# A graph network on one core: layer 1 loads its slot rows and block places in halves of a group instead of quarters

## The chip, the cores and the metric

The kernel runs on one core of a Trainium2 chip. The metric is the device time of one execution in microseconds. The engines named below are TensorE (PE; PEld is its weight load), VectorE (DVE), ScalarE (ACT), GpSimd (POOL) and SyncE (SP), which here only issues DMAs.

## The reference

Two graph layers over 12,500 nodes of 32 channels and 400,000 edges, sorted by destination. Layer 0 weighs each source row with nine spline coefficients from the edge's two attributes and with `weight`, and takes the mean over a node's edges; layer 1 weighs it with four coefficients from the edge's type and sums. After each layer the input is added and the row normalised.

```python
def reference(x, src, dst, edge_attr_2, edge_type_8, ...):
    # layer 0
    messages = einsum('ek,ei,kio->eo', basis(edge_attr_2), x[src], weight)
    out = zeros.at[dst].add(messages) / max(degree, 1)[:, None]
    x = layernorm(x + out + x @ root_w.T + root_b)
    # layer 1
    out = sum over b of segment_sum((x[src] @ W[b]) * etw[b][edge_type][:, None], dst)
    return layernorm(x + out)
```

## The kernel before

The edges are cut into 125 groups of 2304 (`NG`, `GE`) and a rest of near tiles. In a first phase (to about 690 us) each group's edges are sorted by source, so that the rows of one stretch of 896 nodes (a block: 7 windows of 128 nodes) lie next to one another. There are `NBL` = 14 blocks in a group. For every block the sort leaves two things in DRAM: a row of 608 int16 slot numbers (`slots`: which node of the window a slot wants) and a place (`begin_d`, written by `counted`: where the block's rows go among the group's 2304 edges).

Then each layer (`layer(0)`, `layer(1)`) runs over the groups. `take(g)` fetches a group's source rows without a gather, block by block:

- `block(k)` loads, at the first block of each of four `PIECES` of 3, 4, 3 and 4 blocks, the piece's slot rows into `sl`, broadcast to 128 partitions (L1312, on SP's queue), and its places into `hd` (L1316, SP's queue as well). ScalarE loads the places into registers (L1318, a TENSOR_LOAD).
- VectorE compares `sl` with the partition's number and makes the one-hot `s` of the piece (L1324).
- TensorE multiplies seven windows of node rows with `s` into one of three PSUM banks (L1334), 98 matmuls a group.
- ScalarE copies the bank to its place in `yt`, at an offset that it takes from the registers (L1341), 14 copies a group.

`use(g, yt)` of the group before runs between the blocks, in three parts of six chunks. `product`: TensorE turns the rows (`y`, L1354, six matmuls), VectorE makes a one-hot of the destination (`hot`, L1366) and the row times its coefficients (`outer`, `last[0]`, L584 through the helper). `add`: TensorE adds them up in `agg` (L1389, six calls, two instructions each in f32), `LAG` = 2 parts later in layer 1. The sums go to `rows` through ScalarE (`agg_sb`, L603; `rows`, L591 and L593) and small matmuls (L609), and into the nodes in `some` (L743, L746). `Near` takes the rest of the edges by gathers on GpSimd (L124, `n_xg`) and matmuls (`n_bank`, L1083), in units of up to 28 gathers, spread over the groups.

Buffers: `srcs` holds 4 `sl` in layer 1 (2 in layer 0), `heads` 2 `hd`, `onehots` 5 `s` in layer 1, `prods` 4 `hot` and `products` 4 `outer`. The `y` of two parts and the column numbers that `hot` reads lie in one PSUM bank.

The order of the instructions on each engine is not that of the source: when the program is built, a scheduler lays out every engine's queue by priorities and assumed durations, within the dependences and the few orders that the source sets (`tc.issue_after`). Each engine, and SP's queue of DMAs, then works through its queue in order.

Of the kernel before, what the change touches and what calls it, by code (L numbers as in the profile page):

```python
# [11 lines left out]
I16 = mybir.dt.int16  # L12
I32 = mybir.dt.int32
# [4 lines left out]
P = 128  # L18
# [4 lines left out]
def kernel(  # L23
# [38 lines left out]
    nc = tc.nc  # L62
# [3 lines left out]
    CH, NG, G0 = 18, 125, 33  # L66
# [29 lines left out]
    NBL = NW // B  # L96
# [13 lines left out]
    dram = ctx.enter_context(tc.tile_pool(name="dram", bufs=1, space=bass.MemoryType.DRAM))  # L110
# [21 lines left out]
    sort = phase0.enter_context(tc.tile_pool(name="sort", bufs=1))  # L132
# [45 lines left out]
    row = const.tile([P, 1], F32)  # L178
# [47 lines left out]
    def wide(name="wg"):  # L226
        return node_ps.tile([P, 4 * P], F32, name=name)
# [216 lines left out]
    WS = off_[B]  # L444
# [11 lines left out]
        signs(src_16, thr[:NG, w:w + 1], -1.0, counts[:NG, w:w + 1])  # L456

    PIECES = [(k * NBL // 4, (k + 1) * NBL // 4) for k in range(4)]
    PB = max(k1 - k0 for k0, k1 in PIECES)
    PW = PB * WS  # L460
    assert PB <= 4
    PAD = 512
    begin_d = dram.tile([NG, NBL, 4], I32, name="begin_d")
    seg = dram.tile([NG * NBL, 2], F32, name="seg")
    ROWS = TG * NBL
    NT = (NG + TG - 1) // TG
# [11 lines left out]
    def counted():  # L478
        nc.vector.tensor_scalar(counts[:NG, 1:NW], counts[:NG, 1:NW], 0.5, GE / 2, op0=ALU.mult,
                                op1=ALU.add)  # L480
        nc.vector.memset(counts[:, :1], 0.0)
        nc.vector.memset(counts[:, NW:], float(GE))
        out_, t = [sort.tile([P, NBL, B], F32, name=n) for n in ("outside", "rel_to")]
        far = sort.tile([P, 2], F32, name="far")
        firsts, ends = [counts[:NG, i:i + NW].rearrange("g (b j) -> g b j", j=B) for i in (0, 1)]
        anchors = firsts[:, :, BL:BL + 1].to_broadcast([NG, NBL, B])

        for c, to, f, op in ((firsts, out_, lo, ALU.is_lt), (ends, t, hi, ALU.is_gt)):
            nc.vector.tensor_tensor(to[:NG], c, anchors, op=ALU.subtract)
            nc.vector.tensor_tensor(to[:NG], to[:NG],  # L490
                                    f[:NG, None, :].to_broadcast([NG, NBL, B]), op=op)
        nc.vector.tensor_tensor(out_[:NG], out_[:NG], t[:NG], op=ALU.add)
        nc.vector.tensor_reduce(far[:NG, :1], out_[:NG].rearrange("g b j -> g (b j)"), axis=AX.X, op=ALU.add)
        far_ps = wide()
        nc.tensor.matmul(far_ps[:1, :1], far[:NG, :1], ones[:NG, :1], start=True, stop=True)
        nc.vector.tensor_tensor(unfit, unfit, far_ps[:1, :1], op=ALU.add)
        place = sort.tile([P, NBL], F32, name="place")
        nc.vector.tensor_tensor(place[:NG], firsts[:, :, 0], firsts[:, :, BL], op=ALU.subtract)
        nc.vector.tensor_scalar(place[:NG], place[:NG], float(AHEAD), 0.0, op0=ALU.add, op1=ALU.max)
        nc.vector.tensor_scalar(place[:NG], place[:NG], float(AHEAD), None, op0=ALU.min)  # L500

        nc.vector.scalar_tensor_tensor(place[:NG], firsts[:, :, 0], float(BANK), place[:NG],
                                       op0=ALU.mult, op1=ALU.add)
        p_i = sort.tile([P, NBL, 4], I32, name="p_i")
        nc.gpsimd.memset(p_i, 0)
        for k0, k1 in PIECES:
            n = k1 - k0
            nc.vector.tensor_copy(p_i[:NG, k0:k1, :n],
                                  place[:NG, None, k0:k1].to_broadcast([NG, n, n]))
        nc.sync.dma_start(begin_d.rearrange("g b i -> g (b i)"),  # L510
                          p_i[:NG].rearrange("g b i -> g (b i)"))
        sg = sort.tile([P, NBL, 2], F32, name="sg")
        nc.vector.tensor_scalar(sg[:NG, :, 0], firsts[:, :, BL], edges[:NG], None, op0=ALU.add)
        nc.vector.tensor_copy(sg[:NG, :, 1], node[:NG, :NW:B])
        nc.vector.tensor_scalar(sg[:NG, :, 1], sg[:NG, :, 1], row[:NG], None, op0=ALU.subtract)
        nc.sync.dma_start(seg.rearrange("(g b) i -> g (b i)", b=NBL),
                          sg[:NG].rearrange("g b i -> g (b i)"))
        nc.vector.memset(begin, 0.0)
        for t in range(NT):
            n = min(ROWS, NG * NBL - t * ROWS)  # L520
            nc.sync.dma_start(begin[:n, t, :], seg[t * ROWS:t * ROWS + n, :])
# [652 lines left out]

    def layer(which):

        NSRC, NONE, NOUT, LAG, NSUM = ((2, 3, 3, 1, 14), (4, 5, 4, 2, 18))[which]
        KK = K if which == 0 else NB
        GF = G0 if which == 0 else 0
        parts = x3[which][0]  # L1180
        with ExitStack() as stack:
            srcs = stack.enter_context(tc.tile_pool(name="srcs", bufs=NSRC))
# [3 lines left out]
            heads = stack.enter_context(tc.tile_pool(name="heads", bufs=2))  # L1186
# [112 lines left out]
            def take(g):  # L1299

                yt = yts[g % NYT]
                begins = {}
                ones_of = {}

                def block(k):
                    for k0, k1 in PIECES:
                        if k == k0:
                            n = (k1 - k0) * WS
                            sl = srcs.tile([P, PW], I16, name="sl")
                            r0 = g % TG * NBL  # L1310
                            a = slots[g // TG][r0 + k0:r0 + k1, :]
                            nc.sync.dma_start(sl[:, :n], bass.AP(tensor=a.tensor, offset=a.offset,  # L1312
                                                                 ap=[[0, P], [1, n]]))

                            hd = heads.tile([1, 4], I32, name="hd")
                            nc.sync.dma_start(hd, begin_d[g:g + 1, k0, :])  # L1316
                            with tc.issue_after(moves[-2].ins) if len(moves) > 1 else ExitStack():
                                _, v = nc.values_load_multi_w_load_instructions(  # L1318
                                    hd[:, :k1 - k0], engines=[mybir.EngineType.Activation],
                                    min_val=0, max_val=GE * BANK + AHEAD,  # L1320
                                    skip_runtime_bounds_check_because="counted, and bounded")
                            begins.update(zip(range(k0, k1), v))
                            s = ones_.tile([P, PW], BF16, name="s")
                            nc.vector.tensor_scalar(s[:, :n], sl[:, :n], row, None,  # L1324
                                                    op0=ALU.is_equal)
                            for i in range(k0, k1):
                                ones_of[i] = s[:, (i - k0) * WS:]
                    s = ones_of.pop(k)
                    bank = banks[(g * NBL + k) % len(banks)]
                    for j in range(B):  # L1330
                        a, b = at_[j]
                        w = k * B + j

                        nc.tensor.matmul(bank[:, AHEAD + a:AHEAD + b], parts[:, w * M3:w * M3 + P],  # L1334
                                         s[:, off_[j]:off_[j + 1]], start=(j == 0),
                                         stop=(j == B - 1), skip_group_check=True)
                    v = begins.pop(k)
                    to, place = [nc.s_assert_within(
                        e, 0, top, skip_runtime_bounds_check_because="counted, and bounded")
                        for e, top in ((v >> 9, GE), (v & (BANK - 1), AHEAD))]  # L1340
                    moves.append(nc.scalar.activation(  # L1341
                        yt[:M3, ds(to, LONG)], bank[:M3, ds(place, LONG)], AF.Copy))
                return [lambda k=k: block(k) for k in range(NBL)], yt

            def use(g, yt):
# [77 lines left out]
            for g in range(GF, NG + 1):  # L1423
# [6 lines left out]
                n, m = len(new), len(left)  # L1430
# [68 lines left out]
    for c in range(0, CH, 4):  # L1499
        n = min(4, CH - c)  # L1500
# [11 lines left out]
    ends[0][2].append(fallen)  # L1512
    phase0.close()
    layer(0)
    phase1.close()
    ends[1][2].append(near_fits)
    layer(1)
    again = const.tile([1, 1], I32)
    nc.vector.tensor_scalar(again, unfit, 0.5, None, op0=ALU.is_gt)
# [157 lines left out]
```

## Time and profile before

| | |
|---|---|
| median of 12 runs | 3684.37 us (3674.16 to 3696.37) |
| the profiled execution | 3690.56 us, span 3688.5 us |
| granted TensorE clock, mean | 0.915 |
| busy share of the span: PE, PEld, DVE, ACT, POOL | 78%, 67%, 82%, 58%, 70% |
| layer 0 | about 700 to 2300 us |
| layer 1 | about 2310 to 3650 us |
| `sl` loads | 868: 434 of 608 KB, 434 of 456 KB |
| `hd` loads | 868 |

The rows of the profile name line, engine, operation, what is written and what is read. "Idle before" is time in which the engine did nothing before the instruction, and the name behind the arrow is what ended it. An idle engine that is not the bound costs nothing.

### The profile page before, as it was taken

Reading aid. Unit: us, or ns where it says so; the run is one execution under the profiler, and the core shown is the slowest. Engines: PE = TensorE matmul, PEld = TensorE weight load, DVE = VectorE, ACT = ScalarE, POOL = GpSimd, SP = SyncE. Lnnn points to the kernel's source line nnn. Section 1 sums busy time; section 2 is a strip of 40 time slices with the busy share of each in tenths; the row PEclk is TensorE's granted clock in tenths of the full one; section 3 lists DMA queues with packets and bytes.
Section 4 is the critical chain, followed back from the end, with each engine's and each line's share of the span. In section 5 each row is a group of like instructions: output and inputs, shape, how many; then the busy total and the mean of one; then the engine's idle time right before and its main releaser. Section 6 shows DMA issues by size and latency. Waiting matters only on the chain.

```text
span 3688.5 us, 112981 instructions
## 1 busy us (share of the span) xinstructions
PE 2859.7 (78%) x40674; PEld 2463.0 (67%) x40674; DVE 3008.9 (82%) x5850; ACT 2145.3 (58%) x5610; POOL 2590.1 (70%) x2395
## 2 busy tenths in 40 slices
PE   2222221159999999999999998889999999999997
PEld 1121111147877787777777776788888888888886
DVE  5899989579999998887777776678888788888886
ACT  4688866336666665555565654455555555555553
POOL 4767777727777777777777773577777777777730
PEclk9995555579999999999999998899999999999998
DMA  4000000145555555554555544577777676777662
GB/s 94 14 11 14 14 14 14 31 165 173 171 167 174 170 175 154 160 165 148 157 165 154 154 153 150 174 221 228 227 230 222 215 225 220 225 226 229 215 219 89
DMA packets 266157, 565.07 MB, mean 153 GB/s; under 512 B 83608, under 2 KB 149756, under 8 KB 265086
## 3 DMA queue, kind: packets, MB, share of 16 engines
q1 hardware_dynamic: 187288, 511.82, 41.3%
q0 software_dynamic: 75888, 40.38, 7.9%
q8 instruction: 319, 5.23, 0.6%
q10 hardware_dynamic: 2410, 5.59, 0.6%
q14 instruction: 252, 2.06, 0.2%
HBM read 531.77 MB, written 25.78 MB: 151 GB/s over the span
## 4 chain that ended last, share of the span: by engine, by line
PE 45%; POOL 13%; issue 7%; DVE 7%; ACT 5%; DMA 3%; ACTq 1%; SPq 0%; DVEq 0%; POOLq 0%
PE agg L1389 23%; PE bank L1334 15%; POOL n_xg L124 13%; ACT yt L1341 3%; PE y L1354 2%; DVE outer L584 2%; PE n_bank L1083 2%; DMA n_xg<-in_x_dram,n_idx 1%; PE wg L880 1%; DVE s L1324 1%; DVE hot L1366 1%; PE n_sum L746 1%; PE wg L609 1%; ACT agg_sb L603 1%; DVE hot L1376 1%
## 5 line engine op out<-in xcount | busy, mean ns | idle before, releaser
L124 POOL DMA_INDIRECT n_xg<-in_x_dram,n_idx x1469 | 1638.0, 1115 | 559.5 <-issue 433.1
L1341 ACT ACTIVATE yt<-bank x3038 | 1163.5, 383 | 544.0 <-PE bank L1334 244.7
L1389 PE MATMUL agg<-hot,outer 128*128 128x82 f32 (+1 forms) x7812 | 1400.6, 324 | 9.3 <-DVE hot L1376 8.6
L1334 PE MATMUL bank<-s,x 128*128 128x108 bf16 (+3 forms) x21266 | 1162.0, 202 | 103.7 <-ACT yt L1341 70.7
L124 POOL DMA_INDIRECT n_xg<-z_dram,near_i x875 | 921.4, 1053 | 365.8 <-issue 258.5
L1389 PEld LDWEIGHTS agg<-hot,outer 128*128 128x128 f32 (+1 forms) x7812 | 1070.6, 182 | 136.0 <-DVE hot L1376 11.4
L1334 PEld LDWEIGHTS <-x 128*128 128x128 bf16 x21266 | 997.2, 98 | 235.3 <-issue 144.9
L1324 DVE TENSOR_SCALAR s<-sl,row 128x1824 bf16<-128x1824 int16 x868 | 687.5, 792 | 188.1 <-PE bank L1334 161.3
L1376 DVE TENSOR_TENSOR hot<-agg,hot_b 128x984 f32<-128x984 f32 x276 | 325.5, 1179 | 124.7 <-ACT agg_sb L603 52.8
L584 DVE TENSOR_TENSOR outer<-co,y 128x768 f32<-128x768 f32 x375 | 354.7, 946 | 0.0
L1083 PE MATMUL n_bank<-n_w,n_xg 128*32 128x72 f32 x3024 | 145.3, 257 | 214.0 <-DMA n_xg<-in_x_dram,n_idx 111.1
L1366 DVE TENSOR_TENSOR hot<-in_order,y 128x492 f32<-128x492 bf16 x375 | 248.3, 662 | 54.4 <-PE y L1354 47.9
L1354 PE MATMUL y<-add,yt 96*128 96x32 bf16 x3906 | 245.5, 177 | 59.3 <-DVE outer L584 58.2
L1083 PEld LDWEIGHTS n_bank<-n_w,n_xg 128*32 128x32 f32 x3024 | 84.7, 122 | 260.8 <-DMA n_xg<-in_x_dram,n_idx 131.3
L1374 ACT ACTIVATE hot<-hot_b 128x492 f32<-128x492 bf16 x276 | 167.5, 607 | 138.8 <-PE agg L1389 107.2
L1354 PEld LDWEIGHTS <-yt 96*128 96x128 bf16 x3906 | 194.3, 97 | 76.5 <-issue 71.1
L245 ACT ACTIVATE in_order<-src,thr 125x2304 bf16<-125x2304 int16 x97 | 214.0, 2206 | 0.7
L584 DVE TENSOR_TENSOR outer<-co_b,y 128x384 f32<-128x384 f32 x276 | 151.0, 547 | 24.3 <-ACT outer L1373 23.3
L603 ACT ACTIVATE agg_sb<-agg 128x82 f32<-128x82 f32 (+1 forms) x217 | 64.5, 297 | 177.7 <-PE agg L1389 166.1
L1066 DVE TENSOR_TENSOR n_w<-n_basis,n_hot 128x864 f32<-128x864 f32 x162 | 137.3, 850 | 17.6 <-PE n_bank L1083 16.0
L1263 DVE SCALAR_TENSOR_TENSOR co<-eq,etw_sb,co 128x180 f32<-128x180 f32 (+1 forms) x364 | 128.8, 392 | 2.0
L743 DVE TENSOR_SCALAR n_hit<-cols,place_of 82x128 bf16<-82x128 f32 (+2 forms) x301 | 99.3, 341 | 23.0 <-PE n_sum L746 21.5
(267 smaller groups left out, 2851.3 us busy)
## 6 DMA issues: line engine op xcount, KB each, us to landing
sl<-slots SPq DMA_DIRECT2D x434, 608.0 KB
sl<-slots SPq DMA_DIRECT2D x434, 456.0 KB
n_xg<-in_x_dram,n_idx POOLq DMA_INDIRECT x1469
n_xg<-z_dram,near_i POOLq DMA_INDIRECT x875
hd<-begin_d SPq DMA_DIRECT2D x868, 0.0 KB
z_dram<-n_z SPq DMA_DIRECT2D x49, 256.0 KB
co_d<-co SPq DMA_DIRECT2D x13, 360.0 KB
co<-co_d SPq DMA_DIRECT2D x13, 360.0 KB
```

Of the source, the lines that this page charges most:

```text
L124: return nc.gpsimd.indirect_dma_start(out=xg, out_offset=None, in_=table, in_offset=bass.IndirectOffsetOnAxis(ap=idx, axis=0))
L245: nc.scalar.activation(t, of[:NG], AF.Sign, bias=bias, scale=scale, accum_out=total)
L584: return nc.vector.tensor_tensor(t[:, :c, at:at + k * D].rearrange("p c (k d) -> p c k d", k=k), co[:, :, :, None].to_broadcast([P, c, k, D]),
L1083: nc.tensor.matmul(o, self.xg[i][:, at[0], at[1], :], v, start=True, stop=True, tile_position=(0, j * D))
L1324: nc.vector.tensor_scalar(s[:, :n], sl[:, :n], row, None, op0=ALU.is_equal)
L1334: nc.tensor.matmul(bank[:, AHEAD + a:AHEAD + b], parts[:, w * M3:w * M3 + P], s[:, off_[j]:off_[j + 1]], start=(j == 0), stop=(j == B - 1) ...
L1341: moves.append(nc.scalar.activation(yt[:M3, ds(to, LONG)], bank[:M3, ds(place, LONG)], AF.Copy))
L1354: nc.tensor.matmul(y[:, c, :], yt[:M3, k * P:(k + 1) * P], add3[:M3, :], start=True, stop=True)
L1366: nc.vector.tensor_tensor(hot.rearrange("p c (m i) -> p c m i", i=2), rel.to_broadcast([P, SUB, MAXR // 2, 2]), (col_ps if which else col_ ...
L1374: nc.scalar.activation(spread[:, :, 0, :], hot, AF.Copy)
L1376: nc.vector.tensor_tensor(spread[:, :, 1:, :], b0[:, :, :, None].to_broadcast([P, SUB, 2, MAXR]), hot[:, :, None, :].to_broadcast([P, SUB, ...
L1389: near.behind = nc.tensor.matmul(agg[0], t[:, c, :], v, start=(k == 0), stop=(k == CH - 1)).ins
```

## The change

`begin_d` holds each block's place once, instead of a row of four for each block. `LOADS` gives the pieces in which a layer loads: the four `PIECES` in layer 0, two halves of seven blocks in layer 1. In layer 1 one `sl` is 4256 wide, with 2 buffers in place of 4 of 2432; one `hd` has seven places, and one TENSOR_LOAD puts seven values into registers. The one-hots `s` are still made for each of the four pieces, out of the half's `sl`.

```diff
     PIECES = [(k * NBL // 4, (k + 1) * NBL // 4) for k in range(4)]
+    LOADS = PIECES, [(0, NBL // 2), (NBL // 2, NBL)]
...
-    begin_d = dram.tile([NG, NBL, 4], I32, name="begin_d")
+    begin_d = dram.tile([NG, NBL], I32, name="begin_d")
...
-        p_i = sort.tile([P, NBL, 4], I32, name="p_i")
-        nc.gpsimd.memset(p_i, 0)
-        for k0, k1 in PIECES:
-            n = k1 - k0
-            nc.vector.tensor_copy(p_i[:NG, k0:k1, :n],
-                                  place[:NG, None, k0:k1].to_broadcast([NG, n, n]))
-        nc.sync.dma_start(begin_d.rearrange("g b i -> g (b i)"),
-                          p_i[:NG].rearrange("g b i -> g (b i)"))
+        p_i = sort.tile([P, NBL], I32, name="p_i")
+        nc.vector.tensor_copy(p_i[:NG], place[:NG])
+        nc.sync.dma_start(begin_d[:, :], p_i[:NG])
...
-        NSRC, NONE, NOUT, LAG, NSUM = ((2, 3, 3, 1, 14), (4, 5, 4, 2, 18))[which]
+        NSRC, NONE, NOUT, LAG, NSUM = ((2, 3, 3, 1, 14), (2, 5, 4, 2, 18))[which]
...
-                    for k0, k1 in PIECES:
+                    for k0, k1 in LOADS[which]:
                         if k == k0:
                             n = (k1 - k0) * WS
-                            sl = srcs.tile([P, PW], I16, name="sl")
+                            sl = srcs.tile([P, max(b - a for a, b in LOADS[which]) * WS], I16, name="sl")
...
-                            hd = heads.tile([1, 4], I32, name="hd")
-                            nc.sync.dma_start(hd, begin_d[g:g + 1, k0, :])
+                            hd = heads.tile([1, NBL // 2], I32, name="hd")
+                            nc.sync.dma_start(hd[:, :k1 - k0], begin_d[g:g + 1, k0:k1])
...
                             begins.update(zip(range(k0, k1), v))
+                            slots_of.update({i: sl[:, (i - k0) * WS:] for i in range(k0, k1)})
+                    for k0, k1 in PIECES:
+                        if k == k0:
+                            n = (k1 - k0) * WS
                             s = ones_.tile([P, PW], BF16, name="s")
-                            nc.vector.tensor_scalar(s[:, :n], sl[:, :n], row, None,
+                            nc.vector.tensor_scalar(s[:, :n], slots_of[k][:, :n], row, None,
                                                     op0=ALU.is_equal)
```

More of the change, by code (lines that the diff above doesn't have):

```diff
@@ L1302, in take @@
                 begins = {}
-                ones_of = {}
+                ones_of, slots_of = {}, {}
                 def block(k):
-                    for k0, k1 in PIECES:
+                    for k0, k1 in LOADS[which]:
                         if k == k0:
                             n = (k1 - k0) * WS
-                            sl = srcs.tile([P, PW], I16, name="sl")
+                            sl = srcs.tile([P, max(b - a for a, b in LOADS[which]) * WS], I16, name="sl")
                             r0 = g % TG * NBL
```

## The prediction

> **What bounds the kernel now.** I read the page's 40 slices first, then busy times by stage, then the waits of layer 1, then one group in order of time. Only layer 1 (from about 2310 us on) can move: the change does not touch the work of layer 0, and in the built program the order of layer 0's instructions on TensorE, VectorE and ScalarE stays as it is. The busy times by stage (columns: stretch, length, busy of PE, weight loads, VectorE, ScalarE, GpSimd with instruction counts, granted clock, DMA share, GB/s):
>
> ```profile
> 2450.00:2800.00 350.00, 323.38 (x5750) 308.78 (x5749) 289.00 (x517) 199.49 (x593) 264.65 (x252) 1.00 0.73 227
> 2800.00:3300.00 500.00, 456.19 (x8069) 434.64 (x8065) 406.59 (x744) 281.61 (x831) 381.91 (x363) 0.99 0.71 221
> ```
>
> TensorE is busy 92% here and is the bound, at full clock; VectorE 82%, ScalarE 57%, DMA 72%. So what is to be had or lost is TensorE's last 8%. Who waits for whom from 2450 to 3600 us (us in total, times, longest):
>
> ```profile
> DVE s L1324 <- PE bank L1334: 123.8, 164, 2.3
> ...
> PE y L1354 <- DVE outer L584: 47.5, 58, 1.3
> ```
>
> No row has VectorE waiting for a slot load: the loads that the change enlarges are hidden today. TensorE waits 47.5 us for the VectorE product `outer`, and in the groups of instructions its bank matmuls wait another 40.1 us for the ScalarE copy (`ACT yt`). One group in order of time shows the first of the two:
>
> ```profile
> 3005.79 0.94 DVE L1324 TENSOR_SCALAR s<-sl,row 128x2432 bf16<-128x2432 int16 x1 [1.21 <-PE bank L1334]
> ...
> 3006.48 0.30 PE L1354 MATMUL y<-add,yt 96*128 96x32 bf16 x6
> ...
> 3006.83 0.67 DVE L1366 TENSOR_TENSOR hot<-in_order,y 128x492 f32<-128x492 bf16 x1
> ...
> 3007.41 0.95 DVE L584 TENSOR_TENSOR outer<-co,y 128x768 f32<-128x768 f32 x1
> ...
> 3008.41 0.20 PE L1354 MATMUL y<-add,yt 96*128 96x32 bf16 x2 [0.65 <-DVE outer L584]
> ```
>
> The one-hot `s` sits idle 1.21 us until an old bank matmul frees its buffer (five buffers, all full), then `hot` and `outer` follow, and the next `y`, which writes the PSUM bank that they read, waits for them. From the end of one `y` (3006.78) to the next (3008.41) it is 1.63 us, the 0.67 + 0.95 and the hand-overs; TensorE has less work than that in between, here 14 bank matmuls and some small ones. Next, the loads on SP's queue and the register loads on ScalarE's:
>
> ```profile
> 3000.69 0.32 SPq L1312 DMA_DIRECT2D sl<-slots  x1
> ...
> L1318 ACTq TENSOR_LOAD <-hd x432: 310/544/738, 2450.5 to 3597.9; - x144
> ...
> 3010.80:3011.40 0.60, 0.60 (x18) 0.59 (x15) 0.60 (x3) 0.36 (x1) 0.57 (x1) 1.00 0.98 372
> ```
>
> The `s` before that load ended at 3000.67: the buffer's release starts the load at once. The register load is 0.31 us at least and 0.74 at most; taken apart, a piece of four values costs 0.31 and a piece of three 0.70. The last line is a stretch inside a load that was issued at 3009.34: DMA 98% busy at 372 GB/s.
>
> **The change, part by part.**
>
> Set-up: four casts into `p_i` (0.15 us each, near 626 us) become one, and a 0.14 us GpSimd memset at 15 us goes. At best 0.45 us; VectorE is the busy engine there. I take -0.5.
>
> Slot loads: per group four loads of 456 or 608 KB become two of 1064 KB, the bytes the same. From issue to first packet is 0.95 us in the trace, and first to last packet of an undisturbed load 2.3 us (456 KB) or 2.5 us (608 KB). At 372 GB/s the 1,089,536 bytes take 2.9 us; with a tail as seen I estimate 3.3, so 4.3 us from issue to data. Lower end: 3.4, as short as today's. Upper end: the two present loads one behind the other, 2.3 + 2.5 + 0.95 = 5.8 us.
>
> Their start: in the built order of SP's queue `hd` of one half now stands ahead of the next half's `sl`, and with two `heads` buffers that `hd` waits for the register load of two halves earlier. `sl` therefore starts at that register load's end plus 0.3 us instead of at the release of `s`. In today's timeline that is 2.9 us (median) after the `s` that frees the buffer, and the first `s` of the new half comes 7.0 us after it: 3.8 us left for 4.3. That would be 0.5 us too late in every half, if VectorE's order stayed. It does not stay.
>
> Register loads: two of seven values in place of four of three or four; a load of seven is not in the trace. Bounds: 0.70 us (as three values) to 1.5 us (0.31 and six more words at 0.19 each, the slope from one to three). I take 1.0, a load of four and one of three (0.31 + 0.70). Behind it on ScalarE stand the copies; TensorE has at least 2.07 us of work from the block before such a load to the block that needs the copy behind it, and copy + load + copy are 0.38 + 1.0 + 0.38 = 1.8. Cost 0 on the path, at 1.5 us about 5 us over the layer.
>
> The order: the program's builder lays every engine's queue out anew, and that is the largest term. TensorE's order around a group's second `y` (number of instructions; b bank, a agg, y, o other):
>
> ```
> before  b245 x14, y x6, b245 x7, o x6, y x6, ...
> after   b245 x14, y x6, b245 x14, b246 x14, a x5, y x6, ...
> ```
>
> I laid the work between one `y` and the next out with rows of the chain of waits (a bank matmul 0.042 us, an agg 0.23, a y 0.03). Before, 110 of 125 groups have less than 1.70 us of it at the second `y`, 88 us short in sum, of which 47.5 us in 108 groups are seen as waits. After, 7 are short, by 2.8 us in sum. So the wait of `y` for `outer` goes: 47.5 x 125/108 = 55 us.
>
> What is late next is ScalarE. TensorE now does its bank matmuls in longer runs: the bank of three blocks ago is wanted again after less than 0.8 us of work 467 times, before 237 times. Upper price: today's 40.1 x 125/108 = 46 us over 237 places is 0.20 us each, 230 more are 45 us. Lower price 0: from 3010.4 to 3011.8 a run of 28 ran without a listed wait. I take 19 us, nearer to the run.
>
> The slot load in the new order: `hot` and `outer` now stand ahead of more of the `s`. Laid on the same work, from register-load end + 0.3 us + load + `s` + `hot` + `outer` to the `y` that needs them, 95% of the halves have 0.3 us or more to spare at a load of 4.3 and a register load of 1.0. Cost 0. With both together at 6.3 us it is 16 us in sum, at 6.8 us 54, at 7.3 us 116; the upper ends together (5.8 + 1.5) are 7.3.
>
> A rule against the change: the Trainium skill, "DMA: Bandwidth & Descriptors", section "Measured (HBM→SBUF, 128 partitions, SWDGE, issued from GpSimd)", gives 6.15 us for moving 1 MB; by that the load with its first 0.95 us and a 1.0 us register load is 8.1 us, and the sum ends some 200 us slower; the loads of this trace, on another queue, are much shorter, so the rows decide. The same page, "Latency and other measured facts", puts a floor of about 600 ns under a register load; the trace has 0.31 us for four values.
>
> Sum: -55 - 0.5 + 19 = -36 us against the profiled execution (3690.56 us, span 3688.5), which is 6.2 us over the median of the runs shown (3684.37). So 3648 us.
>
> A limit on more: GpSimd's gathers run almost without a break from 2336 to 3541 us (790 in the window, 1.06 us each and 0.30 of issue). Those of the last full unit of 28 end at 3533, its matmuls come at 3579. TensorE can gain 46 us before it waits for them, some 70 if GpSimd's own waits for TensorE (22 us) go too.
>
> **The rivals.**
>
> Late loads, slower. Load and register load together take 6.8 us rather than 5.3: VectorE stops at the first `s` of a half and everything behind it, `hot` and `outer` above all, is late. For it: SP's new chain through `hd`, two buffers only. Against: no wait for a slot load today, and the new order. Price 54 us against the 36: 3684 + 18 = 3702; it turns at about 6.6 us.
>
> ScalarE takes it all back, no change. The runs of bank matmuls cost 0.20 us at each new place (45 us) and the longer register load 5 to 10: -55 + 53 = -2, 3682 us. For it: 0.40 us of copy for 0.29 us of bank matmuls. Against: the run of 28 shown.
>
> The change does nothing: loads were hidden and stay so, and the built order acts on the chip as the old one, because `y` waits less for `outer` only where something else is late: 3684 us. Against it speak the 110 short places.
>
> **How the numbers follow.** Gain as summed 0.60 (own range 3614 to 3672), no change by either way 0.14, late loads 0.26. The range's low end is the gain with GpSimd's limit, 3684 - 70; its high end the late loads at 6.9 us (between 54 and 116, some 65): 65 - 36 = 29 over the median. A change under 0.2% (7 us) is about what a measurement of this kernel can't tell from none.
>
> **What would show it.** Right: the wait of `y` for `outer` falls from 47.5 us to under 10, TensorE's busy share in 2450 to 3300 rises to about 94%, no row of VectorE waiting for `sl`, the register load near 1.0 us, bank matmuls waiting for `ACT yt` about 60 us. Wrong: VectorE's `s` waiting for the DMA `sl` in most groups, a register load of 1.5 us, or `n_bank` waiting for the gathers.

## The result and the profile after

The changed kernel takes 3723.69 us (median of 10 runs, 3714.93 to 3738.43) against 3685.78 us beside it (40 runs): a ratio of 1.0107, with a 95% interval of 1.0095 to 1.0119. It is 38 us slower where 36 us less were forecast, and lies 11 us over the upper end of the range. The profiled execution took 3717.78 us, span 3715.7.

The busy times by stage, same stretches and columns as in the prediction:

```profile
2450.00:2800.00 350.00, 316.96 (x5529) 299.82 (x5529) 274.66 (x498) 185.72 (x569) 253.87 (x237) 1.00 0.71 217
2800.00:3300.00 500.00, 453.97 (x7869) 430.02 (x7868) 391.90 (x717) 263.01 (x809) 381.35 (x354) 0.99 0.70 216
```

TensorE is busy a little less than before (91% against 92%, not the 94% forecast) and gets through fewer matmuls in the same time (7869 against 8069). Who waited for whom from 2450 to 3600 us (us in total, times, longest):

```profile
ACT agg_sb L599 <- PE agg L1389: 140.4, 94, 2.8
...
ACT yt L1341 <- issue: 105.9, 99, 1.4
PE bank L1334 <- ACT yt L1341: 98.8, 110, 1.7
DVE s L1324 <- PE bank L1334: 79.8, 77, 4.6
...
DVE s L1324 <- DMA sl<-slots: 10.0, 13, 1.8
```

Three of these rows before:

```profile
ACT yt L1341 <- issue: 50.0, 79, 1.2
...
ACT agg_sb L603 <- PE agg L1389: 44.6, 83, 2.3
PE bank L1334 <- ACT yt L1341: 40.1, 123, 1.0
```

The row of `y` waiting for `outer`, 47.5 us before, is not in the list any more: that part came as forecast. In its place TensorE's bank matmuls wait 98.8 us for ScalarE's copy `yt` (40.1 before), ScalarE waits 140.4 us at `agg_sb` for the last agg matmul (44.6 before), and 105.9 us pass ahead of copies with nothing but "issue" (50.0 before). A register load isn't counted as busy, so it shows as "issue". Its own row:

```profile
L1314 ACTq TENSOR_LOAD <-hd x210: 956/966/1240, 2450.3 to 3597.1; - x105
```

A load of seven values takes 0.97 us, close to the forecast (1.0). Where it stands is seen in the chain that ended last; a stretch like this one comes once in most groups (start, duration, engine and line):

```profile
2810.57 0.52 PE agg L1389 x4
...
2811.11 0.24 ACT agg_sb L599
2811.35 0.73 ACTq L1314
2812.08 0.06 issue
2812.14 0.07 ACTq L1341
...
2812.39 0.39 ACT yt L1341
...
2812.83 0.44 PE bank L1334 x7
```

From the end of the group's last `agg` (2811.09) ScalarE runs `agg_sb`, the register load (0.73 plus the hand-over to the address registers) and one copy, one behind the other, and only then is the next bank free for TensorE (2812.83): 1.74 us. ScalarE's rows around it, in order of time, show what it did ahead of that:

```profile
2811.11 0.24 ACT L599 ACTIVATE agg_sb<-agg 128x82 f32<-128x82 f32 x1 [1.45 <-PE agg L1389]
...
2812.39 0.80 ACT L1341 ACTIVATE yt<-bank  x2 [1.05 <-issue]
```

It stood idle for 1.45 us with the next copies behind `agg_sb` in its queue. So TensorE enters the stretch with one free bank: its seven matmuls start at 2811.09, the two `wg` follow at 2811.40, and then it waits. Over all of layer 1 the trace has this in 107 groups: TensorE's work ends 0.66 us (median) after the last `agg`, and its next bank matmul starts 1.75 us after it.

TensorE's idle time per group, taken from the same trace by what it ran before and after each gap, moved so: between `wg` (the small matmul on `agg_sb`) and the next bank matmul 0.051 to 0.886 us; between two bank matmuls 0.306 to 0.060; ahead of `y` 0.436 to none. Times 125 groups that is +104, -31 and -55 us. The net is small, and it isn't the whole loss. Layer 1 is 34 us longer in the profiled executions (1418.9 to 1453.2 us): TensorE's idle time there grows by 7 us in all, from 139 to 146, and the time that the profile shows as busy by 27 us, from 1270 to 1296.

Most of that is bank matmuls. They take 47.5 ns in the mean instead of 45.2 (98 x 125 of them: 28 us). A bank's seven matmuls, a block, take 0.28 us when they run without a break. After the change 448 blocks in layer 1 take about 0.41 us and start 0.05 us after the end of a copy, without any listed wait; before there were 198. They run at the pace of ScalarE's copies. Each matmul's record is some 0.2 us long and the records overlap, so 0.13 us without a start between two blocks shows as busy and not as a wait. Two runs of the trace after, of three and of four blocks:

```profile
3016.45 1.01 PE L1334 MATMUL bank<-s,x 128*128 128x108 bf16 x21
...
3018.16 1.41 PE L1334 MATMUL bank<-s,x 128*128 128x108 bf16 x28
```

The fourth block makes the second run 0.40 us longer and not 0.28: it starts 0.42 us after the third, just behind a copy. The run of 28 before that the prediction read as free of waits is as long, for the same reason:

```profile
3010.50 1.41 PE L1334 MATMUL bank<-s,x 128*128 128x108 bf16 x28
```

In sum such blocks cost 59 us more than at 0.28 us each, before 24. Stops, behind which the first block takes 0.44 us, became fewer (196 to 146). The clock records show a little more time at half clock: 18.8 us lost between 2400 and 3640 us, before 6.8.

### The profile page after: what moved, and what is told of

The parts are those of the page before. It is cut to its first block, busy times and chain, and to the rows that moved or that the text cites. A ratio compares the mean times of both kernels' runs of the same rounds, so it can differ in the third digit from the quotient of the medians.

```text
span 3715.7 us, 111562 instructions
## 1 busy us (share of the span) xinstructions
PE 2885.6 (78%) x40674; PEld 2477.2 (67%) x40674; DVE 2997.4 (81%) x5847; ACT 2118.9 (57%) x5610; POOL 2601.1 (70%) x2394
## 4 chain that ended last, share of the span: by engine, by line
PE 51%; POOL 8%; issue 5%; DVE 5%; ACT 4%; DMA 3%; ACTq 3%; SPq 0%; DVEq 0%; POOLq 0%
PE agg L1389 26%; PE bank L1334 19%; POOL n_xg L124 8%; ACT yt L1341 2%; ACTq L1314 2%; PE y L1354 2%; DMA sl<-slots 2%; PE n_bank L1079 1%; PE wg L876 1%; DMA n_xg<-in_x_dram,n_idx 1%; DVE s L1324 1%; ACT agg_sb L599 1%; ACTq L1341 1%; PE wg L1105 1%; DVE hot L1376 1%
## 5 line engine op out<-in xcount | busy, mean ns | idle before, releaser
L1389 PE MATMUL agg<-hot,outer 128*128 128x82 f32 (+1 forms) x7812 | 1417.9, 324 | 12.8 <-DVE hot L1376 10.8
L1334 PE MATMUL bank<-s,x 128*128 128x108 bf16 (+3 forms) x21266 | 1176.8, 202 | 170.6 <-ACT yt L1341 140.0
L1334 PEld LDWEIGHTS <-x 128*128 128x128 bf16 x21266 | 1012.4, 99 | 317.7 <-issue 202.5
L124 POOL DMA_INDIRECT n_xg<-z_dram,near_i x875 | 941.1, 1076 | 384.7 <-issue 258.4
L1354 PE MATMUL y<-add,yt 96*128 96x32 bf16 x3906 | 222.8, 178 | 1.1 <-DVE outer L580 0.9
L1354 PEld LDWEIGHTS <-yt 96*128 96x128 bf16 x3906 | 182.7, 98 | 10.7 <-issue 5.8
```

The lines of the kernel that those rows point to most:

```text
L124: return nc.gpsimd.indirect_dma_start(out=xg, out_offset=None, in_=table, in_offset=bass.IndirectOffsetOnAxis(ap=idx, axis=0))
L1354: nc.tensor.matmul(y[:, c, :], yt[:M3, k * P:(k + 1) * P], add3[:M3, :], start=True, stop=True)
L1389: near.behind = nc.tensor.matmul(agg[0], t[:, c, :], v, start=(k == 0), stop=(k == CH - 1)).ins
```

## The experiments

Three theories. **One**: the register load of seven values stands on ScalarE in series with `agg_sb` and the next copies, while TensorE has no bank left. **Two**: slot loads come late, because they are larger and have two buffers, or because `hd` stands ahead of them in SP's queue. **Three**: the new order with longer runs of bank matmuls overruns ScalarE's copies by itself.

The table has, beside each median and its ratio to the kernel before on the same chip, the length of layer 1 in the profiled execution (from its first bank matmul to the end of the span) and waits between 2450 and 3600 us.

| kernel | median us | ratio | layer 1 us | register loads of a group, us | bank for yt | y for outer | s for sl |
|---|---|---|---|---|---|---|---|
| before | 3685.78 | | 1418.9 | 0.70, 0.31, 0.70, 0.31 | 40.1 | 47.5 | none |
| changed | 3723.69 | 1.0107 | 1453.2 | 0.97 twice | 98.8 | none | 10.0 |
| places in halves alone | 3716.85 | 1.0082 | 1444.7 | 0.97 twice | 93.3 | none | none |
| slots in halves alone | 3954.92 | 1.0720 | 1706.9 | 0.70, 0.31, 0.70, 0.31 | 46.7 | 90.8 | 2.7 |
| four `hd` | 3731.13 | 1.0116 | 1457.3 | 0.97 twice | 99.7 | none | 9.9 |
| places two blocks early | 3731.91 | 1.0121 | 1459.9 | 0.97 twice | 88.4 | 2.1 | 11.7 |
| places four blocks early | 3802.36 | 1.0321 | 1530.6 | 0.97 twice | 119.8 | 2.9 | 11.9 |
| eight values a load | 3689.18 | 1.0004 | 1416.3 | 0.55 twice | 62.8 | 10.4 | 27.5 |
| two loads of four | 3660.05 | 0.9932 | 1392.0 | 0.31 four times | 80.0 | 13.8 | 10.8 |
| changed, agg_sb on VectorE | 3662.62 | 0.9924 | 1403.9 | 0.97 twice | 22.6 | 12.9 | 45.3 |
| before, agg_sb on VectorE | 3642.22 | 0.9889 | 1366.5 | 0.70, 0.31, 0.70, 0.31 | 21.0 | 46.4 | none |
| before, four values a load | 3630.31 | 0.9842 | 1377.8 | 0.31 four times | 29.6 | 28.1 | none |
| both on before | 3616.58 | 0.9826 | 1364.2 | 0.31 four times | 21.4 | 41.5 | none |
| both on changed | 3640.02 | 0.9884 | 1370.6 | 0.31 four times | 68.9 | 17.3 | 21.6 |

**One part of the change at a time.** Places in halves alone:

```diff
-        NSRC, NONE, NOUT, LAG, NSUM = ((2, 3, 3, 1, 14), (2, 5, 4, 2, 18))[which]
+        NSRC, NONE, NOUT, LAG, NSUM = ((2, 3, 3, 1, 14), (4, 5, 4, 2, 18))[which]
...
                     for k0, k1 in PIECES:
                         if k == k0:
                             n = (k1 - k0) * WS
+                            sl = srcs.tile([P, PW], I16, name="sl")
...
-                            nc.vector.tensor_scalar(s[:, :n], slots_of[k][:, :n], row, None,
+                            nc.vector.tensor_scalar(s[:, :n], sl[:, :n], row, None,
```

> Only the places are loaded in halves (seven values); the slot rows are loaded in quarters with four buffers as before. In the built order 101 groups have the register load between agg_sb and the next bank copy, and 11 y are short of work ahead. Theory 1: as slow as the changed kernel, 3710 to 3730, bank waiting for yt about 95 us. Theory 2: the loss goes away, and with the wait of y gone as well 3640 to 3665. Theory 3: 3710 to 3730.

Slot rows in halves alone:

```diff
-                            hd = heads.tile([1, NBL // 2], I32, name="hd")
-                            nc.sync.dma_start(hd[:, :k1 - k0], begin_d[g:g + 1, k0:k1])
+                    for k0, k1 in PIECES:
+                        if k == k0:
+                            hd = heads.tile([1, 4], I32, name="hd")
+                            nc.sync.dma_start(hd, begin_d[g:g + 1, k0, :])
```

> Only the slot rows are loaded in halves (two buffers); the places are loaded in quarters, three or four values, as before. In the built order 14 groups have a register load between agg_sb and the next copy, but 134 y are short of work ahead (146 us in sum; before: 111 and 88). Theory 1: no loss from the register load, the wait of y for outer is back with 50 to 80 us, 3680 to 3710. Theory 2: VectorE's s waits for sl in many halves, 3715 or more. Theory 3: 3675 to 3690, the runs are short again.

The places alone give 3716.85 us (ratio 1.0064 to 1.0101), most of the loss, with no wait for a slot load: as Theory 1 had it, and Theory 3 too. The slots alone give 3954.92 us, 245 us over the upper end that Theory 1 had. Theory 2's open range (3715 or more) holds it, but not for Theory 2's reason: slot loads aren't late there. The last packet lands 4.2 us (median) ahead of the `s`, and `s` waits 2.7 us for them in all. The built order puts `y` close behind `y` in 134 groups, 146 us short by the prediction's way of counting (88 before), `y` waits 90.8 us for `outer`, and the windows of the trace show the clock (the column after GpSimd's):

```profile
2450.00:2800.00 350.00, 303.95 (x4694) 283.49 (x4694) 241.98 (x432) 163.06 (x488) 208.77 (x199) 0.91 0.61 186
2800.00:3300.00 500.00, 435.01 (x6360) 404.88 (x6359) 326.12 (x582) 218.85 (x654) 289.70 (x281) 0.87 0.58 176
```

0.87 where the changed kernel has 0.99; 138 us go with it between 2350 and 3600 us. The longer waits and the clock together make most of the loss against the changed kernel. The records at half clock come 13.7 us apart in long rows there (at 2484.5, 2498.2, 2511.8 and 2525.5 us, for instance), which is the length of a group (1706.9 / 125) and four times 3.4 us, the length of the shortest records: a stop that comes at the same place of each group then falls at the same place of a stretch of 3.4 us, group after group. That this is why the clock falls so often in this order fits, but no run took it apart. This kernel therefore doesn't price the slot loads.

**More `hd` buffers**, against Theory 2's second half (SP's queue held by `hd`):

```diff
-            heads = stack.enter_context(tc.tile_pool(name="heads", bufs=2))
+            heads = stack.enter_context(tc.tile_pool(name="heads", bufs=2 + 2 * which))
```

> The changed kernel with four buffers for hd in layer 1 in place of two, so that hd, and with it the next slot load in SP's queue, no longer waits for the register load of two halves earlier. 112 groups have the register load between agg_sb and the next copy. Theory 1: as slow as the changed kernel, 3710 to 3735, though the SP queue's wait for the register load (495 us before) falls below 100. Theory 2: most of the loss goes, 3680 to 3700. Theory 3: as the changed kernel.

3731.13 us: no gain. The trace of the changed kernel says why: from the end of the `s` that frees a buffer to the issue of the next `sl` it is 0.03 us in 95 of 100 halves. So `hd` delays no slot load.

**The register load moved away.** Both kernels load a half's places some blocks ahead of its first block (`EARLY` = 2, then 4):

```diff
                 def block(k):
+                    if which and k in (NBL // 2 - EARLY, NBL - EARLY):
+                        h, k0 = divmod(k + EARLY, NBL)
+                        if g + h < NG:
+                            places(g + h, k0, k0 + NBL // 2)
```

> The changed kernel with one edit: the seven places of a half are loaded into ScalarE's registers two blocks earlier, so that in the built order no register load stands between the copy of agg (agg_sb) and the next copy of a bank (after: 106 of 125 groups). Slot loads in halves with two buffers as in the changed kernel; TensorE's spacing of the y stays as there (3 short places). Theory 1 (the 0.97 us register load behind agg_sb on ScalarE holds TensorE up, about 1 us a group): TensorE's bank matmuls wait about 45 us for yt in 2450 to 3600 instead of 98.8, y still waits under 5 us for outer, and the time is 3640 to 3665 us, under the kernel before. Theory 2 (slot loads come late, with two buffers and hd ahead of them in SP's queue): no change, 3715 to 3730. Theory 3 (longer runs of bank matmuls overrun ScalarE's copies): no change either, 3710 to 3730.

> The changed kernel, with each half's places loaded four blocks before its first block. In the built order the register load of seven (0.97 us) then stands behind agg_sb in 1 group instead of 106, and 23 y are close to the one ahead, 7.3 us short in sum. Theory 1, if what counts is agg_sb, register load and copy in one series: the wait for yt falls from 98.8 to 40 to 60 us, 3650 to 3685 us. If, as two blocks earlier, the load only comes to stand a few copies further back in a ScalarE queue that is short of time over the whole stretch after the last agg: the wait for yt stays at 85 us or more, 3700 to 3735 us. Theory 2 (slot loads of 1064 KB, 5.3 us from issue to last packet, 2.1 us ahead of the s that needs them): 10 us or so of waits for sl in either case.

3731.91 us, and 3802.36 us (ratio 1.0301 to 1.0341): Theory 1 in its simple form, that the load must only not be the neighbour of `agg_sb`, falls twice. The chain of the second kernel:

```profile
2893.20 1.19 PE agg L1399 x10
2894.41 0.25 ACT agg_sb L600
2894.67 0.39 ACT yt L1351
...
2895.37 0.18 ACT rows L588
2895.55 0.33 ACT yt L1351
2895.89 0.59 ACTq L1302
...
2896.84 0.40 ACT yt L1351
...
2897.28 0.44 PE bank L1344 x7
```

The load has gone three copies back in ScalarE's queue, and the series behind the last `agg` has only become longer: `agg_sb`, three copies, `rows`, register load, copy, 2.9 us from 2894.39 to 2897.28. What counts is not the neighbour but everything that ScalarE still has to do between the last `agg` and the copy that TensorE needs next. Why four blocks early is 70 us worse than two, which neither side of the expectation had, is in part this length (2.5 us with two blocks). Of the 56 us by which TensorE is idle longer in layer 1, 51 lie between a `y` and the next bank matmul; this wasn't taken apart further.

**The load made shorter at its place.** Eight values in the changed kernel's load, the eighth unused; in the built order it stands behind `agg_sb` in 113 groups:

```diff
-                            hd = heads.tile([1, NBL // 2], I32, name="hd")
+                            hd = heads.tile([1, 8], I32, name="hd")
...
-                                    hd[:, :k1 - k0], engines=[mybir.EngineType.Activation],
+                                    hd[:, :8 if which else k1 - k0], engines=[mybir.EngineType.Activation],
```

> The changed kernel, with register loads of eight values instead of seven (the eighth place is not used). A load of eight took 0.55 us in the trace from the chip on which everything was 1.7 times as long, a seven 0.97 us. The load stays where it is: in the built order it stands behind agg_sb in 113 groups (106 in the changed kernel). Theory 1: TensorE's idle time between the wg matmuls and the next bank, 0.886 us a group in the changed kernel, falls by about the 0.42 us by which the load is shorter, to 0.4 to 0.55 us; in this built order 93 of the y are close to the one ahead again (60.7 us short in sum), so that y's wait for outer may be back at up to 30 us; 3670 to 3700 us. If the load's length is not on the path, the idle time behind wg stays over 0.8 us a group, 3715 us or more.

3689.18 us (1.0004, 0.9982 to 1.0025), inside what Theory 1 gave. The same stretch of the chain as in the changed kernel:

```profile
2804.46 0.70 PE agg L1396 x6
...
2805.18 0.24 ACT agg_sb L601
2805.42 0.32 ACTq L1321
...
2806.05 0.39 ACT yt L1348
...
2806.49 0.44 PE bank L1341 x7
```

0.32 where 0.73 stood, and 1.33 us from `agg` to bank instead of 1.74. The idle time between `wg` and bank falls from 0.886 to 0.53 us a group, and layer 1 by 37 us; 113 x 0.42 = 47 us was to be had at most. Part of the rest is visible: `s` now waits 27.5 us for slot loads instead of 10.0, and blocks at the pace of copies don't become fewer (502).

**Loads of four.** The changed kernel with a half's places in two loads of four values, and the kernel before with four values in each of its loads:

```diff
+                    if k in hd_of:
+                        places(hd_of.pop(k)[:, 4:8], k)
...
+                                places(hd[:, :4], k0)
+                                hd_of[k0 + 4] = hd
```

```diff
-                                    hd[:, :k1 - k0], engines=[mybir.EngineType.Activation],
+                                    hd[:, :4], engines=[mybir.EngineType.Activation],
```

> The changed kernel (slot rows in halves, two buffers), but the seven places of a half, padded to eight, go into ScalarE's registers by two loads of four values, at the half's first and fifth block. A load of four takes 0.31 us in the trace of before. In the built order a register load stands behind agg_sb in 9 groups, as before, and 125 of the y are closer than 1.70 us to the one ahead, 73.9 us short in sum, as before. Theory 1: the wait for yt falls from 98.8 us to about 40 us, y's wait for outer is back at about 40 us, and the time is that of before or a little under, 3665 to 3695 us. Theory 2: the slot loads are the same as in the changed kernel, so the time stays at 3710 us or more, with VectorE's s waiting for slot loads.

> The kernel before, with every register load taking four values (the fourth of a three-block piece is not used). If the time of a load hangs on the number of values as before's trace has it (four 0.31 us, three 0.70 us), every load now takes 0.31 us, and ScalarE has 250 x 0.39 = 97 us less to do in layer 1. Theory 1: only the part that stands behind agg_sb or between two copies that TensorE waits for comes off the path: the wait for yt falls from 40 us to 20 to 30 us and the time to 3660 to 3680 us. Theory 3: the copies themselves are the wait, so the time stays at 3680 to 3690 us.

3660.05 us (0.9916 to 0.9949) and 3630.31 us (0.9825 to 0.9859): better than Theory 1 had it, both times, and Theory 2's 3710 us and Theory 3's 3680 to 3690 us fall. One sign of Theory 1 failed: with two loads of four the wait for `yt` is still 80.0 us, not about 40. Yet layer 1 is 61 us shorter than in the changed kernel, 53 of it in time that the profile shows as busy: 246 blocks at the pace of copies in place of 448, and no record at half clock between 2450 and 3600 us. So the listed wait alone doesn't measure what ScalarE costs. The register loads of the second kernel in layer 1:

```profile
L1318 ACTq TENSOR_LOAD <-hd x444: 303/308/376, 2451.3 to 3598.2; - x148
```

All at 0.31 us, also those of layer 0, where layer 1's first bank matmul now comes at 2254 us (2248 us in the kernel with both edits) and in all others at 2262 to 2273. So 41 of its 56 us are layer 1's and some 15 layer 0's: the register loads of three values at 0.70 us had been a cost before the change, in both layers.

**agg_sb on VectorE**, which takes the wait for the last `agg` off ScalarE's queue:

```diff
         def copy():
-            nc.scalar.activation(s[:k, :n * MAXR], agg, AF.Copy)
+            if layer:
+                nc.vector.tensor_copy(s[:k, :n * MAXR], agg)
+            else:
+                nc.scalar.activation(s[:k, :n * MAXR], agg, AF.Copy)
```

> The changed kernel, with layer 1's copy of agg into agg_sb (one per group, 82 values a partition) done by VectorE instead of ScalarE. ScalarE's queue then holds nothing that waits for the last agg matmul: the copies of the banks run as their banks are done, and the register load of seven values (0.97 us) has no agg_sb ahead of it. Theory 1 (ScalarE is held by agg_sb until the last agg matmul ends, and agg_sb, bank copies and the 0.97 us register load then stand in series while TensorE has no bank left): the wait of bank matmuls for yt falls from 98.8 us to under 50 us, and the time to 3640 to 3680 us. Theory 2 (slot loads come late): nothing in the loads is changed, so 3710 to 3735 us. Theory 3 (the longer runs of bank matmuls overrun ScalarE's copies by themselves, 0.40 us a copy against 0.29 us of matmuls): the wait for yt stays over 80 us, 3700 to 3730 us. If VectorE, which is busier than ScalarE, is now the one held by the last agg, s, hot and outer are late, the wait of y for outer is back at over 40 us, and the time is above 3680 us.

> The kernel before, with the same one edit as the run ahead of it: layer 1's agg_sb copied by VectorE. In the kernel before a register load stands behind agg_sb in 9 of 125 groups only. Theory 1: little to gain, the wait of bank matmuls for yt falls from 40 us to about 30 and y's wait for outer stays near 45 us, 3670 to 3690 us; so the edit is worth clearly less here than on the changed kernel. If the edit is worth as much here (40 us and more), agg_sb on ScalarE is a cost of its own and not one that the register load makes.

The changed kernel falls to 3662.62 us (0.9899 to 0.9949). Its waits:

```profile
DVE s L1327 <- DMA sl<-slots: 45.3, 46, 2.8
...
PE bank L1337 <- ACT yt L1344: 22.6, 40, 1.8
...
PE y L1357 <- DVE outer L580: 12.9, 26, 1.6
```

The wait for `yt` goes from 98.8 to 22.6 us with the same register loads of 0.97 us: the load costs where it stands in series behind the last `agg`. Theory 3 falls as the cause of the listed wait, since ScalarE has the same copies to make. A share of it stays: 377 blocks still run at the pace of copies (49 us), against 197 (25 us) with the same edit on the kernel before; how much of that the order makes, and how much the longer loads, was not separated. And now slot loads are late, 45.3 us, the second cause in sight. But on the kernel before the same edit brings 44 us (3642.22 us, 0.9873 to 0.9906), more than Theory 1 had: `agg_sb` on ScalarE is a cost of its own there too, and the long register load makes it larger (61 us on the changed kernel).

**Both edits on both kernels**, to see what the slot loads cost when ScalarE is out of the way:

> The kernel before (quarters, four slot buffers) with both edits that made it faster: four values in every register load (-56 us alone) and agg_sb copied by VectorE (-43 us alone). If they take away the same wait (ScalarE's series after the last agg): 3620 to 3635 us, little under the better of the two. If they are separate costs: about -99 us, 3585 to 3605 us. I take 3615 us, with the wait for yt under 20 us.

> The same two edits on the changed kernel: slot rows in halves with two buffers, the places of a half by two loads of four values, agg_sb copied by VectorE. It differs from the run ahead of it by the slot loads alone. Theory 1 alone: with ScalarE out of the way the halves cost nothing, and the time is within 10 us of that run. Theory 2 as second cost: a load of 1064 KB lands about 2 us ahead of its s instead of 6 us, and with TensorE faster it lands too late; VectorE's s waits for sl by 20 us or more, and the time is 20 to 40 us over that run.

With quarters 3616.58 us (0.9804 to 0.9848), the fastest of all and 71 us under the kernel before beside it (3688.02); its interval overlaps that of four values a load alone. The two edits aren't separate costs: together they bring 71 us, and 56 and 44 alone. With halves 3640.02 us (0.9867 to 0.9902), with these waits:

```profile
PE bank L1355 <- ACT yt L1362: 68.9, 97, 1.1
...
DVE s L1345 <- DMA sl<-slots: 21.6, 27, 1.6
```

The 23 us between them looked like Theory 2's second cost. But the halves kernel still has loads of three values in layer 0, and starts layer 1 20 us later (2268.3 against 2247.9 us); in layer 1 itself the two differ by 6 us (1370.6 and 1364.2). Together with the 8.5 us between the changed kernel and the one with quarters of slots, the larger slot loads come to 6 to 9 us. The halves kernel with layer 0 mended too, beside the quarters kernel:

> The changed kernel with slot rows in halves and two buffers, layer 1's places by two loads of four values, agg_sb copied by VectorE, and now layer 0's register loads with four values too (0.31 us instead of 0.70 for the pieces of three). From the profiled runs, layer 1 took 1370.6 us with halves and 1364.2 us with quarters, both mended, and layer 0 ended 20 us earlier where its loads have four values. If the larger slot loads are the smaller cause: 3620 to 3627 us, 3 to 12 us over the quarters kernel beside it. If they cost the 20 to 40 us that the second theory gave them: 3636 us or more.

> The kernel before with four values in every register load and agg_sb copied by VectorE, beside the run ahead of it: 3616 us as measured, within 5 us.

These two ran on a chip on which everything is 1.7 times as long: 6095.05 and 6097.90 us, before 6137.89. On another such chip first runs of four kernels of the table had fallen: eight values 6139.84, four blocks early 6252.83, both edits on before 6143.49, on changed 6143.27, before 6182.87. On both the mean granted clock is 0.74 and TensorE is idle for two fifths of layer 1; before and both edits differ by under 1%, and halves and quarters are equal there (6143.27 and 6143.49, 6095.05 and 6097.90). It speaks for a small cost of the larger slot loads, but doesn't size it at full clock.

## Why the prediction was wrong

By its own steps:

- **The order, `y` for `outer`** (-55): right in kind and size. The wait is gone; -55 us in the idle time ahead of `y`.
- **A register load of seven values takes 1.0 us**: right, 0.97.
- **"Cost 0 on the path, at 1.5 us about 5 us"**: this is the step that failed; the register load was put at nothing on the path. The prediction held copy + load + copy (1.8 us) against the work that TensorE has from the block before the load (2.07 us at least). But ScalarE doesn't begin that series when the block before is done. It is held at `agg_sb` until the last `agg` ends, and what TensorE has left from there to the block that needs the copy is 0.65 us (median, counted in the built order with the prediction's own rows). The series from there is `agg_sb` 0.24, load and hand-over, copy 0.39: 1.74 us in the chain. In the built order the load stands between `agg_sb` and the next copy in 106 groups, before in 9. So 1.74 - 0.65 = 1.09 us in 97 more groups, 106 us; the idle time there grew by 104 us. The trace after has the same two times, 0.66 and 1.75 us. All of this could be had from the built order and rows of the trace before; the prediction asked of every register load what lies around it, and didn't ask what holds ScalarE ahead of it.
- **ScalarE late next** (+19): right in kind, too small. Blocks that follow the pace of the copies went from 198 to 448, much as counted (237 to 467 places), at 0.13 us each (0.41 for 0.28 us) where the upper price had 0.20: +35 us. The lower price, 0, rested on a run of 28 matmuls without a listed wait. That run had an unlisted one: its fourth block starts 0.41 us after the third, 0.05 us after a copy. The listed wait for `yt` grew by 58.7 us beside this, through the failed step: without `agg_sb` on ScalarE it is 22.6 us, less than before.
- **The slot load** (3.3 us from first to last packet, 4.3 from issue, cost 0): too short. The packet records have 4.43 and 5.4 us (medians; before, with the packets sorted by load size, 2.9 and 3.9 us for 456 KB, 3.5 and 4.5 us for 608 KB), 246 GB/s and not the 372 that one stretch showed; other transfers run beside them. The last packet lands 2.0 us ahead of the first `s` that reads it, 5.4 us before. Load and register load together are 6.4 us; at 6.3 the prediction's own count gave 16 us; the waits show 10.0, and the runs a cost of 6 to 9 us.
- **Their start behind `hd`**: didn't happen; four `hd` gain nothing. Late loads, the rival that was priced as the slower case, is thus a small part of the loss, by size of the load alone.
- **The set-up** (-0.5): not measurable; layer 1 starts between 2262 and 2273 us in kernels that share layer 0.

With the failed step priced, -55 - 31 + 104 and 6 to 9 us of slot loads, the sum is some 25 us slower and not 36 faster. The copies' pace, +35 us more of it, would take the sum past the 38 us measured; fewer stops, shorter `y` and other idle time take most of the difference back, as the totals of layer 1 show (+7 us idle, +27 busy). Of the rivals, "ScalarE takes it all back" named the engine and both of its costs, and priced the register load at 5 to 10 us. That the late loads, 3702 us, came nearest in time is luck: they are the small part.

The clock took a little too. The records at half clock, 3.4 us long or a multiple, are 8 instead of 3 between 2450 and 3600 us. The Trainium skill, "TensorE: Matmul & The Clock Gate", section "Part 1: The HAM clock gate", has the clock set by how busy TensorE was in windows of about 3.4 us. The length of the records agrees, but TensorE needn't stand idle through a whole one: the longest stop in these 1150 us is 1.34 us before and 1.75 us after. In the 14 traces of the table's kernels the clock falls 110 times between 2350 and 3640 us, each time after a stretch of 3.4 us in which TensorE was idle for at least 0.30 of the time. Some 310 such stretches weren't followed by a fall, so this alone doesn't decide it, and no run took the clock by itself.

The page that the prediction weighed, "DMA: Bandwidth & Descriptors" in the section "Measured (HBM→SBUF, 128 partitions, SWDGE, issued from GpSimd)", gives 6.15 us for 1 MB; the trace has 4.43 us for 1.09 MB on this queue, between the prediction's 3.3 and the page.

## What to carry to other kernels

When an instruction gets longer on an engine that isn't the bound, find what holds that engine ahead of it: behind a wait for the bottleneck engine's last result, everything up to the next copy that the bottleneck needs is in series with it, however idle the engine is on average. Compare that series with the work that the bottleneck has from the same moment, in the order as built, not in the source. Look beyond the list of waits: measure how long equal pieces of work take, since short waits can hide in busy time. And look at a cost that scales with a count before making the count larger: here the load of three values, at 0.70 us, was worth more than the whole change.

## What the runs showed of the hardware

- A register load's time doesn't follow the number of values: four took 0.31 us, eight 0.55, three 0.70, seven 0.97. Padding three to four or seven to eight makes it shorter. Other counts weren't run.
- The same matmuls in another order can lose much more to the clock: with slots alone in halves 138 us went to half clock between 2350 and 3600 us, before 7 us. The number of stops doesn't tell it: with four values in each load of the kernel before they are more (239 against 196), and no record at half clock lies between 2450 and 3600 us.
- A bank's seven matmuls that wait for a copy by 0.13 us show as busy time, not as a wait, because the records of the matmuls overlap: 198 times before, 448 after.
- The kernel before took 3686 to 3688 us on three chips and 6138 and 6183 us on two others, at a mean granted clock of 0.74 instead of 0.91. Differences of 2 to 5% between kernels were under 2% there (four blocks early to both edits on before: 5.1% and 1.8%).
